# One attention layer over a graph: the mask merge moved to later steps, edge values on GpSimd, q2/k2 evictions at the end of a step

## The chip, the cores and the metric

The kernel runs on one core of a Trainium2 chip. The metric is the device time of one execution in microseconds (us), median of several runs. A profiled execution of the same program gives the trace that this text reads; its engines are PE (TensorE matmuls; PEld are its weight loads), ACT (ScalarE), DVE (VectorE), POOL (GpSimd) and SP, whose queue issues most transfers.

## The reference

384 nodes with 1024 features; 6528 edges, each with a type. The layer normalises, projects twice (q, k, v, then q2, k2, v2), adds an edge-type mask to the scores of 16 heads and adds its output to the input:

```python
h = jnp.maximum(_layernorm(x, axis=-1), 0.0)
q = h @ wq.T + bq                    # k and v likewise
q2 = (q @ wiq.T + biq).reshape(N, H, D).transpose(1, 0, 2)   # k2, v2 likewise
mask = jnp.full((N, N), -jnp.inf).at[src, dst].set(w[edge_type - 1])
mask = mask.at[idx, idx].set(jnp.where(jnp.isneginf(diag), w[3], diag))
scores = jnp.einsum('hnd,hmd->hnm', q2, k2) * scale + mask[None]
attn = jax.nn.softmax(scores, axis=-1)
out = jnp.einsum('hnm,hmd->hnd', attn, v2).transpose(1, 0, 2).reshape(N, OUT_F)
return x + out @ wo.T + bo
```

Here `w` is the softplus of four edge-type weights. Several edges may fall on one cell of the mask; the last one counts.

## The kernel before, in words

**Precision.** Every float32 operand is kept as a high part and a low part (`hi`, `lo`), and a product is made of three matmuls: hi·hi, hi·lo, lo·hi (`mm3`). So each weight chunk of 128x1024 that is loaded (`load`) is split: ACT copies the high part (`split_hi`, L77) and DVE or POOL subtracts it from the raw chunk for the low part (`split_lo`, L82).

**Weight steps.** There are 56 chunks; a step `w` works on chunk `w`. Steps 0 to 7 make v, 8 to 15 q, 16 to 23 v2, 24 to 31 k (the "k steps", `m` = 0 to 7), 32 to 47 alternate q2 and k2 for the eight pairs of heads, and the last eight chunks belong to the output projection `wo`. At the head of steps 0 to 31 `slot_head(w)` issues, in this order: the high split of chunk w+2, the evictions of the step before (`flush`, which runs what stands in `pend`), the low split of chunk w+2, the low parts that go with the evictions (`post`), the load of chunk w+4. An eviction of v, q or k is `evac_row`: DVE L381 scales the PSUM bank into `f`, ACT L382 writes the high part, DVE L383 the low part. In the k steps `v2_evac` is put into `pend` too: DVE L523, ACT L525, POOL L526. One of the three PSUM banks of tag `g` holds a v2 sum until its `v2_evac`, so that the k steps turn over the other two: step w writes the bank that step w-2 filled, and waits for that step's L381.

**The mask.** The edges are 51 columns of 128. Each edge's cell number is src·384+dst (`key`). So that the last edge of a cell wins, `mask_detect` (DVE L217) compares a column with its own row form and counts later edges on the same cell; `mask_index` (DVE L223, L224) turns cells that are overwritten later into a dump address, for a group of columns at once. `mask_values` makes each edge's value from its type, by nine small operations. `mask_scatter` (POOL L228) writes 128 values into one of three tables in DRAM by an indirect transfer; a table's next scatter waits for the landing of the one before. The detects and three scatters per step are spread over steps 0 to 19. In step 20 POOL reads the tables back (`mask_load`, L238), fills the mask tile `ma` (L140, L142) and writes its diagonal (`mask_base`, L210, L212). `mask_select` (DVE L242) lays one table over `ma`, by a predicated copy of 128x1152.

**Attention.** Steps of attention, `i` = 0 to 47, one for each third of a head, run as a pipeline over the engines. In step i PE makes the scores of i (`do_S`, L679), DVE adds the mask for i-1 (`do_ttr`, L685), ACT takes the exponential of i-2 (`do_exp`, L689), POOL normalises i-3 (`do_norm`, L694), PE transposes i-5 (`do_T`, L699), ACT and DVE evict the transpose of i-6 (`do_pt`, L708, L709), and every third step PE multiplies by v2 (`do_A`, L716), with `do_ao` and `do_aos` behind it (L726, L727, L731, L732). Between these PE is filled with the matmuls of q2 and k2, later with those of wo (`fill`). The work beside those matmuls, split and load of coming chunks and the eviction of a finished one (`qk_head`, `qk_done`: ACT L376, DVE L377, then transfers on SP), is put into a list `tasks`, which `run_tasks` empties once in each attention step. The splits of wo chunks 2 to 7 are issued by `wo_prep` at the ends of the attention steps in `WSTEPS`.

**What sets the order.** The schedule is manual: each engine runs its instructions in the order in which the program issues them, and waits at the first one that isn't ready. An instruction that stands early in the program therefore holds up all that its engine has behind it.

Of the kernel before, what the change touches and what calls it, by code (L numbers as in the profile page):

```python
# [12 lines left out]
OP = mybir.AluOpType  # L13
# [3 lines left out]
EC = E // 128  # L17
# [5 lines left out]
def gnn_kernel(ctx: ExitStack, tc: tile.TileContext, x, edges, erows, etw, wq, wk, wv, wiq, wik, wiv, wo,  # L23
# [6 lines left out]
    nc = tc.nc  # L30
# [6 lines left out]
    ctx.enter_context(tc.manual_schedule())  # L37

    EB = 8
    GI = 3  # L40
    NTAB, RNG = 3, EC // 3
    WARM = 20

    def bank(tag):
# [15 lines left out]
    def load(w):  # L60
        if w >= NCH:
            return
        n, m = chunks[w]
        raw[w] = wpool.tile([128, D], F32, tag="raw", name="raw", bufs=3)
        nc.sync.dma_start(raw[w], W[n][m])

    def split_hi(w, dst=None, dve=False):
        if w >= NCH:
            return
        if dst is None:  # L70
            t = wpool.tile([128, 2, D], F32R, tag="whl", name="whl", bufs=4)
            dst = (t[:, 0, :], t[:, 1, :])
        whl[w] = dst
        if dve:
            nc.vector.tensor_copy(dst[0], raw[w])
        else:
            nc.scalar.activation(dst[0], raw[w], AF.Copy)  # L77

    def split_lo(w, eng=None):
        if w < NCH:  # L80
            hi, lo = whl[w]
            (eng or nc.vector).tensor_tensor(lo, raw[w], hi.bitcast(F32), OP.subtract)  # L82

    def split(w, lo_eng=None, dst=None, hi_dve=False):
        split_hi(w, dst, hi_dve)
        split_lo(w, lo_eng)
# [32 lines left out]
    val = const.tile([128, EC], F32, name="val")  # L119
    idx = const.tile([128, EC], I32, name="idx")  # L120
    w8 = const.tile([128, 12], F32, name="w8")
# [8 lines left out]
    def mask_consts():  # L130
        nc.gpsimd.memset(upper, 1.0)
        nc.gpsimd.affine_select(upper, upper, pattern=[[1, 128]], compare_op=OP.is_gt, fill=0.0, base=0,
                                channel_multiplier=-1)
        nc.gpsimd.iota(dump.bitcast(I32), pattern=[[0, 1]], base=CELLS, channel_multiplier=1)
        nc.gpsimd.tensor_copy(w8[:, 8:9], dump.bitcast(I32))
        nc.gpsimd.memset(zero, 0.0)
# [7 lines left out]
    def table_clear(g):  # L144

        nc.sync.dma_start(tabs[g][:CELLS, :].rearrange("(j p m) o -> p j (m o)", p=128, m=N),
                          zero[:, None, :].to_broadcast([128, NT, N]))

    def mask_floats():
        nc.gpsimd.tensor_copy(ed.bitcast(F32), ed)  # L150

    def mask_keys():
        nc.gpsimd.tensor_scalar(tmpe[:, 0, :], tmpe[:, 0, :], float(N), None, op0=OP.mult)
        nc.gpsimd.tensor_tensor(key, tmpe[:, 0, :], tmpe[:, 1, :], OP.add)
# [5 lines left out]
    def softplus_b():  # L160
        nc.scalar.activation(w8[:, 4:8], w8[:, 4:8], AF.Exp)
        nc.scalar.activation(w8[:, 4:8], w8[:, 4:8], AF.Ln, bias=1.0)

        nc.scalar.activation(sq, epsc, AF.Exp)

    def softplus_c():
        nc.vector.tensor_tensor(w8[:, 4:8], w8[:, 4:8], w8[:, 0:4], OP.add)
        nc.vector.tensor_scalar(w8[:, 4:8], w8[:, 4:8], 8.0, 1.0e-37, op0=OP.mult, op1=OP.max)

    def mask_values():  # L170
        t, ty = tmpe[:, 0, :], tmpe[:, 2, :]
        nc.vector.tensor_scalar(val, ty, 0.0, w8[:, 7:8], op0=OP.is_equal, op1=OP.mult)
        for i in range(4):
            nc.vector.tensor_scalar(t, ty, float(i + 1), w8[:, 4 + i:5 + i], op0=OP.is_equal, op1=OP.mult)
            nc.vector.tensor_tensor(val, val, t, OP.add)

    krt = work.tile([128, N], F32, tag="e", name="kr", bufs=EB)
    kf = ert[:, :2 * EC]
# [1 line left out]
    def key_rows():  # L180

        nc.gpsimd.tensor_copy(kf, er)
        nc.gpsimd.tensor_scalar(kf[:, :EC], kf[:, :EC], float(N), None, op0=OP.mult)
        nc.gpsimd.tensor_tensor(krt[:, :EC], kf[:, :EC], kf[:, EC:], OP.add)
        nc.sync.dma_start(krow.rearrange("c j -> (c j)").rearrange("(p e) -> p e", p=128), krt[:, :EC])
# [10 lines left out]
    def key_load(g, s):  # L196

        if s == 0:
            t = work.tile([128, 2, NT, N], F32R, tag="pt", name="rows")
            krv[g] = t.bitcast(F32).rearrange("p a k n -> p (a k n)")  # L200
        c0, c1 = parts(g)[s]
        dst = krv[g][:, s * PA * 128:(s * PA + c1 - c0) * 128]
        for c in range(c0, c1):
            rows[c] = krv[g][:, (s * PA + c - c0) * 128:(s * PA + c - c0 + 1) * 128]
        nc.sync.dma_start(dst, krow[c0:c1, :].rearrange("c j -> (c j)").partition_broadcast(128))
# [14 lines left out]
    def mask_index(j0, j1):  # L220

        k, n, i, t0 = (a.rearrange("p (r j) -> p r j", r=NTAB)[:, :, j0:j1] for a in (key, cnt, idx, tmpe[:, 0, :]))
        nc.vector.scalar_tensor_tensor(t0, n, 2.0 * CELLS, k, op0=OP.mult, op1=OP.add)  # L223
        nc.vector.tensor_scalar(i, t0, w8[:, 8:9], None, op0=OP.min)  # L224
# [15 lines left out]
    def mask_select(g):  # L240

        nc.vector.copy_predicated(ma, mbt[g].bitcast(I32), mbt[g])  # L242
# [64 lines left out]
    def warm(n):  # L307
        for i in range(n):
            ps = bank("g")
            nc.tensor.transpose(ps[:, :128], ident, ident)  # L310

    mask_consts()
    warm(WARM)
    key_rows()
# [42 lines left out]
    ln_rstd()  # L357
    mask_floats()
    split(1, nc.gpsimd)
    softplus_b()  # L360
    softplus_c()
    mask_keys()


# [20 lines left out]
    w = 0  # L385
    pend, post = [], []

    def flush(last=False):
        while pend:
            pend.pop(0)()  # L390
        while last and post:
            post.pop(0)()

    def slot_head(w):
        split_hi(w + 2)
        if w != 1:
            flush()
        split_lo(w + 2, nc.gpsimd if w in (1, 2) else None)
        while post:
            post.pop(0)()  # L400
        load(w + 4)
# [26 lines left out]

    def detect(s):

        if s == 1:
            mask_values()
        if s < NTAB:
            table_clear(s)
        if 3 <= s < 6:
            key_load(1, s - 3)
        if 7 <= s < 10:
            key_load(2, s - 7)
        detects((0, 3, 6)[s] if s < 3 else 4)
        if s >= 3:  # L440
            scatters(3)
        if s == 14:
            biv_load()
# [3 lines left out]
    def detects(n):  # L447
        for i in range(nde[0], min(EC, nde[0] + n)):
            mask_detect(sc_order[i])
            if i % (NTAB * GI) == NTAB * GI - 1 or i == EC - 1:  # L450
                mask_index(i // (NTAB * GI) * GI, i // NTAB + 1)
            nde[0] = i + 1

    def extra_q(m):
# [4 lines left out]
    def scatters(n):  # L459
        for _ in range(n):  # L460
            if nsc[0] < EC:
                mask_scatter(nsc[0])
                nsc[0] += 1
# [64 lines left out]
    def extra_k(m):  # L528
        if 0 < m <= 6:
            pend.append(lambda: v2_evac(m - 1))  # L530
        for g in {0: (0, 1), 1: (2,)}.get(m, ()):
            mask_select(g)
        if m < 2:
            residual(m + 6)
    kT = gtile("g2")
# [31 lines left out]
    def run_tasks():  # L567
        while tasks:
            tasks.pop(0)()
# [27 lines left out]

    LT, LA = 5, 7
    PRE, RATE, RATE_O, RATE_E = 84, 7.9, 8, 8
    WSTEPS = (37, 38, 41, 44, 47, 51)  # L600
    PAR, OPOOL, ODVE = 1, (2, 3, 6), (2,)

    otile = {}
# [83 lines left out]
    def do_exp(i):  # L687
        s = sts[i]
        nc.scalar.activation(es[i], es[i], AF.Exp, bias=s[:, 0:1], scale=-1.0, accum_out=s[:, 1:2])  # L689
# [39 lines left out]
    def do_aos(h):  # L729
        p = h // 2  # L730
        nc.scalar.activation(ao[:, 0, p, :], aof[p], AF.Copy)  # L731
        nc.gpsimd.tensor_tensor(ao[:, 1, p, :], aof[p], ao[:, 0, p, :].bitcast(F32), OP.subtract)  # L732
# [19 lines left out]
    for i in range(S + LA + 4):  # L752
        now[0] = i
        r = RATE if len(gens) == 2 else RATE_O if i < S else RATE_E
        fill(r / 2)
        if i < S:
            do_S(i)
        fill(r / 2)
        if 0 <= i - 1 < S:
            do_ttr(i - 1)  # L760
        if 0 <= i - 2 < S:
            do_exp(i - 2)
        if 0 <= i - 3 < S:
            do_norm(i - 3)
        run_tasks()
        if 0 <= i - LT < S:
            do_T(i - LT)
        j = i - LA
        if j >= 2 and (j - 2) % 3 == 0 and (j - 2) // 3 < 16:
            do_A((j - 2) // 3)  # L770
        if 0 <= i - LT - 1 < S:
            do_pt(i - LT - 1)
        if j >= 3 and (j - 3) % 3 == 0 and (j - 3) // 3 < 16:
            do_ao((j - 3) // 3)
        if j >= 4 and (j - 4) % 6 == 3:
            do_aos((j - 4) // 3)
        if i == XSTEP:
            assert len(gens) < 2
            xb_load()
        if i in WSTEPS:  # L780
            wo_prep(wp)
            wready[wp] = i + 2
            wp += 1
# [57 lines left out]
```

## Time and profile before

| | us |
|---|---|
| median of 3 runs | 320.03 (319.42 to 320.71) |
| the profiled execution | 318.8 |
| span of its trace | 317.1 |
| PE busy in it | 297.0 (94%) |
| DVE busy | 204.3 (64%) |
| POOL busy | 166.5 (53%) |
| ACT busy | 154.8 (49%) |

The span runs from the first to the last instruction of the program; 1.7 us of the execution's time lie around it. A busy share is an average over stages of different kinds, so that PE's idle 20 us have to be looked for by place. The trace also tells the clock that was granted to PE, as a share of full speed.

### The profile page before, as it was taken

The numbers are of one execution on the slowest core, as the hardware profiler recorded it, in microseconds if no ns is written. First come the engines' busy times: TensorE is split into PE (matmuls) and PEld (weight loads), VectorE is DVE, ScalarE is ACT, GpSimd is POOL, SyncE is SP. The second block draws the span as 40 slices with busy tenths as digits, with TensorE's granted clock in tenths as the row PEclk, the third lists the DMA queues.
The fourth block names the chain that finished last, engine by engine and source line by source line (L and its number), as shares of the span: only waits on it lengthen the run. The fifth ranks groups of instructions, "written<-read, shape, count | busy, mean of one in ns | idle before, by whom it ended". The sixth has DMA issues, their size and how long they took to land.

```text
span 317.1 us, 4954 instructions
## 1 busy us (share of the span) xinstructions
PE 297.0 (94%) x1643; PEld 279.4 (88%) x1643; DVE 204.3 (64%) x494; ACT 154.8 (49%) x286; POOL 166.5 (53%) x163
## 2 busy tenths in 40 slices
PE   6699999999999995499999999999999999699995
PEld 5699999999888894499999999999999898588884
DVE  2979999986534320999933666666565657796413
ACT  3693434533422220255453567686776758676200
POOL 4654567775767666033333347282837365857010
PEclk9599999999999998599999999999999999999999
DMA  7899567545495559233348975647474626900005
GB/s 226 267 271 360 171 208 246 183 136 199 146 291 196 159 177 353 93 137 131 102 144 205 272 199 143 180 113 196 120 193 115 192 64 166 366 34 0 2 0 198
DMA packets 22377, 55.12 MB, mean 174 GB/s; under 512 B 4816, under 2 KB 8400, under 8 KB 22352
## 3 DMA queue, kind: packets, MB, share of 16 engines
q1 hardware_dynamic: 20288, 53.01, 54.6%
q0 software_dynamic: 2064, 1.80, 1.9%
q8 instruction: 13, 0.21, 0.3%
q14 instruction: 12, 0.10, 0.1%
HBM read 40.39 MB, written 4.97 MB: 143 GB/s over the span
## 4 chain that ended last, share of the span: by engine, by line
PE 69%; DMA 12%; issue 6%; POOL 6%; DVE 3%; ACT 3%; SPq 0%; DVEq 0%; POOLq 0%
PE g L366 17%; PE g L368 17%; PE g L367 17%; DMA tab<-val,idx 10%; PE a L716 5%; PE s L679 4%; PE t L699 4%; POOL tab L228 3%; DMA g<-in_x_dram 2%; PE g L412 2%; POOL e L694 1%; ACT nat L376 1%; DVE whl L82 1%; DVE pt L709 1%; ACT e L689 1%
## 5 line engine op out<-in xcount | busy, mean ns | idle before, releaser
L366 PE MATMUL g<-g,whl 128*128 128x384 f32 x312 | 107.3, 344 | 8.2 <-DVE f L381 8.2
L368 PE MATMUL g<-g,whl 128*128 128x384 f32 x312 | 105.3, 337 | 0.0
L367 PE MATMUL g<-g,whl 128*128 128x384 f32 x312 | 105.0, 336 | 0.0
L228 POOL DMA_INDIRECT tab<-val,idx x51 | 58.2, 1141 | 31.5 <-DMA tab<-val,idx 12.1
L366 PEld LDWEIGHTS g<-g,whl 128*128 128x128 f32 x312 | 59.3, 190 | 8.5 <-issue 8.5
L694 POOL TENSOR_TENSOR e<-e,s 128x384 f32<-128x384 f32 x48 | 40.2, 846 | 49.0 <-DVE s L693 43.1
L77 ACT ACTIVATE whl<-raw 128x1024 fp32r<-128x1024 f32 x51 | 53.3, 1049 | 23.3 <-PE g L368 21.1
L367 PEld LDWEIGHTS g<-g,whl 128*128 128x128 f32 x312 | 59.3, 190 | 0.0
L368 PEld LDWEIGHTS g<-g,whl 128*128 128x128 f32 x312 | 59.1, 189 | 0.0
L82 DVE TENSOR_TENSOR whl<-raw,whl 128x1024 fp32r<-128x1024 f32 x39 | 47.6, 1221 | 13.5 <-ACT whl L77 13.5
L382 ACT ACTIVATE g<-f,bc 128x384 fp32r<-128x384 f32 x24 | 14.8, 617 | 65.6 <-DVE f L381 65.6
L82 POOL TENSOR_TENSOR whl<-raw,whl 128x1024 fp32r<-128x1024 f32 x13 | 32.0, 2460 | 17.5 <-ACT whl L77 13.0
L377 DVE SCALAR_TENSOR_TENSOR nat<-g,bc,nat 128x384 fp32r<-128x384 f32 x16 | 9.9, 618 | 36.3 <-ACT nat L376 36.3
L689 ACT ACTIVATE e<-e,s 128x384 f32<-128x384 f32 x48 | 29.4, 613 | 7.8 <-DVE s L685 7.0
L709 DVE TENSOR_TENSOR pt<-t,pt 128x384 fp32r<-128x384 f32 x48 | 26.4, 549 | 4.7 <-ACT pt L708 4.2
L685 DVE CUSTOM_DVE_ANT_0 e<-s,ma 128x384 f32<-128x384 f32 x48 | 26.3, 549 | 4.0 <-PE s L679 3.8
L699 PE MATMUL t<-ident,e 128*128 128x128 f32 x144 | 23.7, 273 | 3.4 <-POOL e L694 2.6
L708 ACT ACTIVATE pt<-t 128x384 fp32r<-128x384 f32 x48 | 23.1, 482 | 6.4 <-PE t L699 5.4
L679 PE MATMUL s<-ks,qs 128*128 128x384 f32 x96 | 25.2, 343 | 0.2
L699 PEld LDWEIGHTS t<-ident,e 128*128 128x128 f32 x144 | 18.2, 140 | 7.7 <-POOL e L694 3.2
L376 ACT ACTIVATE nat<-g,bc 128x384 fp32r<-128x384 f32 x16 | 9.3, 582 | 26.2 <-PE g L368 20.2
L383 DVE SCALAR_TENSOR_TENSOR g<-f,bc,g 128x384 fp32r<-128x384 f32 x24 | 20.9, 872 | 0.8 <-ACT g L382 0.8
(147 smaller groups left out, 431.7 us busy)
## 6 DMA issues: line engine op xcount, KB each, us to landing
ks<-nat SPq DMA_DIRECT2D x32, 192.0 KB, 3.5
raw<-in_wv_dram SPq DMA_DIRECT2D x8, 512.0 KB, 5.6
raw<-in_wq_dram SPq DMA_DIRECT2D x8, 512.0 KB, 3.7
raw<-in_wiv_dram SPq DMA_DIRECT2D x8, 512.0 KB, 3.4
raw<-in_wk_dram SPq DMA_DIRECT2D x8, 512.0 KB, 4.6
raw<-in_wiq_dram SPq DMA_DIRECT2D x8, 512.0 KB, 3.4
raw<-in_wik_dram SPq DMA_DIRECT2D x8, 512.0 KB, 4.7
raw<-in_wo_dram SPq DMA_DIRECT2D x8, 512.0 KB, 4.9
```

The costliest lines, as they stand in the source:

```text
L77: nc.scalar.activation(dst[0], raw[w], AF.Copy)
L82: (eng or nc.vector).tensor_tensor(lo, raw[w], hi.bitcast(F32), OP.subtract)
L228: nc.gpsimd.indirect_dma_start(out=tabs[c // RNG], out_offset=bass.IndirectOffsetOnAxis(ap=idx[:, c:c + 1], axis=0), in_=val[:, c:c + 1], ...
L366: nc.tensor.matmul(ps, lhi, rhi, start=first, stop=False)
L367: nc.tensor.matmul(ps, lhi, rlo, start=False, stop=False)
L368: nc.tensor.matmul(ps, llo, rhi, start=False, stop=last)
L679: nc.tensor.matmul(ps[:, :N], qs[:, o, t * 128:(t + 1) * 128], ks[:, o, s, :], start=(s == 0), stop=(s == 1))
L685: nc.vector.tensor_tensor_reduce(e, st_ps.pop(i)[:, :N], ma[:, t, :], -0.125, 3.0e38, OP.add, OP.min, s[:, 0:1])
L689: nc.scalar.activation(es[i], es[i], AF.Exp, bias=s[:, 0:1], scale=-1.0, accum_out=s[:, 1:2])
L694: nc.gpsimd.tensor_tensor(es[i], es[i], s[:, 2:3].to_broadcast([128, N]), OP.mult)
L699: nc.tensor.transpose(ps[:, k * 128:(k + 1) * 128], es[i][:, k * 128:(k + 1) * 128], ident)
L709: nc.vector.tensor_tensor(lo, pv, hi.bitcast(F32), OP.subtract)
```

## The change

Five edits, in the order of the program:

- The high split of chunk 2 is issued before the operations of the softplus (`softplus_b`), no more at the head of step 0; the two DVE operations of `softplus_c` move into step 0, behind the low split of chunk 2.
- `mask_values` runs on POOL in step 0 (it ran on DVE in step 1), and the low splits of chunks 3 and 4 run on DVE (they ran on POOL).
- The groups of `mask_index` end at columns 1, 3, 5, 8, 11, 14, 17 of each table (they ended at 3, 6, 9, 12, 15, 17), and five detects instead of six belong to step 2.
- `mask_select` for the three tables is issued in k steps 4, 5 and 6 (two were issued in k step 0, one in k step 1).
- `run_tasks` stands behind `do_aos` at the end of an attention step (it stood between `do_norm` and `do_T`). In `WSTEPS` the second and third wo split move from steps 38 and 41 to 40 and 42.

PE's instructions stand in the same order in both kernels.

```diff
-    GI = 3
+    JI = [0, 1, 3, 5, 8, 11, 14, RNG]
...
     def mask_values():
-        nc.vector.tensor_scalar(val, ty, 0.0, w8[:, 7:8], op0=OP.is_equal, op1=OP.mult)
+        nc.gpsimd.tensor_scalar(val, ty, 0.0, w8[:, 7:8], op0=OP.is_equal, op1=OP.mult)
         for i in range(4):
-            nc.vector.tensor_scalar(t, ty, float(i + 1), w8[:, 4 + i:5 + i], op0=OP.is_equal, op1=OP.mult)
-            nc.vector.tensor_tensor(val, val, t, OP.add)
+            nc.gpsimd.tensor_scalar(t, ty, float(i + 1), w8[:, 4 + i:5 + i], op0=OP.is_equal, op1=OP.mult)
+            nc.gpsimd.tensor_tensor(val, val, t, OP.add)
...
     split(1, nc.gpsimd)
+    split_hi(2)
     softplus_b()
-    softplus_c()
...
     def slot_head(w):
-        split_hi(w + 2)
+        if w > 0:
+            split_hi(w + 2)
         if w != 1:
             flush()
-        split_lo(w + 2, nc.gpsimd if w in (1, 2) else None)
+        split_lo(w + 2)
...
     def detect(s):
-        if s == 1:
+        if s == 0:
+            softplus_c()
             mask_values()
...
-        detects((0, 3, 6)[s] if s < 3 else 4)
+        detects((0, 3, 5)[s] if s < 3 else 4)
...
             mask_detect(sc_order[i])
-            if i % (NTAB * GI) == NTAB * GI - 1 or i == EC - 1:
-                mask_index(i // (NTAB * GI) * GI, i // NTAB + 1)
+            if i + 1 == NTAB * JI[1]:
+                mask_index(JI.pop(0), JI[0])
...
-        for g in {0: (0, 1), 1: (2,)}.get(m, ()):
-            mask_select(g)
+        if 4 <= m < 7:
+            mask_select(m - 4)
...
-    WSTEPS = (37, 38, 41, 44, 47, 51)
+    WSTEPS = (37, 40, 42, 44, 47, 51)
...
             do_norm(i - 3)
-        run_tasks()
         if 0 <= i - LT < S:
             do_T(i - LT)
...
             do_aos((j - 4) // 3)
+        run_tasks()
         if i == XSTEP:
```

## The prediction

> **What bounds the kernel now.** I read the page's busy times and slices first, then PE's waits, then the time lines of the engines named there. PE is busy 94% of the span, and its order doesn't change, so only its idle time and its slow clock can be won.
>
> ```profile
> PE   6699999999999995499999999999999999699995
> ...
> PEclk9599999999999998599999999999999999999999
> ```
>
> Each digit is 7.9 us. Beside the first two slices there is one hole, in slices 15 and 16 (119 to 135 us), and the clock falls to half in the same place. Near slice 34 lies a smaller hole. PE's waits name them:
>
> ```profile
> PE g L366 <- DVE f L381: 8.2, 1, 8.2
> ...
> PE t L699 <- POOL e L694: 2.6, 2, 1.7
> ...
> PE t L699 <- DVE pt L709: 0.8, 1, 0.8
> ```
>
> (Columns: us in total, times, longest.) The 8.2 us are one wait of k step 2 for an eviction on DVE. DVE's time line says what DVE did then:
>
> ```profile
> 112.47 1.22 DVE L82 TENSOR_TENSOR whl<-raw,whl 128x1024 fp32r<-128x1024 f32 x1
> 127.14 2.90 DVE L242 COPY_PREDICATED ma<-mbs 128x1152 f32<-128x1152 int32 x2 [13.45 <-POOL ma L212]
> 129.94 0.68 DVE L495 TENSOR_TENSOR xh<-xh,bot 128x512 f32<-128x512 f32 x1
> 130.53 0.55 DVE L381 TENSOR_TENSOR f<-g,rrow 128x384 f32<-128x384 f32 x1
> ```
>
> DVE stood 13.45 us in front of the first mask copy, which waited for POOL's L212; the eviction L381 of k step 0 was ready at 118.7 but queued behind it. POOL in turn came late through its 51 scatters (34.1 to 117.4) and the read-back:
>
> ```profile
> 116.41 0.96 POOL L228 DMA_INDIRECT tab<-val,idx  x1 [0.30 <-issue]
> ...
> 121.71 0.75 POOL L238 DMA_DIRECT2D mbs<-tab  x1 [2.54 <-DMA tab<-val,idx]
> ...
> 126.66 0.45 POOL L212 TENSOR_TENSOR ma<-ma,d 128x128 f32<-128x128 f32 x1
> ```
>
> **The mask copies in k steps 4 to 6.** *Removed:* PE's last matmul before the hole starts at 122.72; at its pace of 0.173 us the next would start at 122.89, and starts at 131.23: 8.34 us. *The clock:* from 131.23 to 135.46 PE starts 13 matmuls at half clock in 4.23 us; at full clock 13 x 0.173 = 2.25, so 1.98 us more. The Trainium skill ("TensorE: Matmul & The Clock Gate", the HAM clock gate) states that an idle window of about 3.4 us halves the clock and a busy one of as much restores it; 3.4 us at half speed would cost 1.7. I take the row, 1.98. Both go only if no new hole of that length comes. Sum 10.3.
>
> *Is the mask ready?* A step is 24 x 0.173 = 4.16 us. Without the hole steps 26, 27, 28 end at 127.05, 131.2, 135.4. The first copy stands on DVE behind the head of k step 4 (step 28), so it is reached at about 135.3, while POOL's L212 was done at 127.1 even at its old pace. An earlier test: the third v2 eviction (L523, head of step 28, reached at 132.0) reuses a buffer that POOL's first L526 must have read, and that stands behind L212: 127.1 + 1.53 = 128.6. So POOL may be 3.4 us later than before without harm.
>
> *Does DVE bear the copies there?* Its work in such a step of before goes from one L381 to the next, 134.08 to 137.84:
>
> ```profile
> 134.08 0.54 DVE L381 TENSOR_TENSOR f<-g,rrow 128x384 f32<-128x384 f32 x1
> ...
> 135.13 1.21 DVE L82 TENSOR_TENSOR whl<-raw,whl 128x1024 fp32r<-128x1024 f32 x1
> 136.27 1.65 DVE L383 SCALAR_TENSOR_TENSOR g<-f,bc,g 128x384 fp32r<-128x384 f32 x1
> 137.84 0.55 DVE L381 TENSOR_TENSOR f<-g,rrow 128x384 f32<-128x384 f32 x1
> ```
>
> L383 takes 1.65 here, but 0.61 at 132.13 where POOL is idle; POOL's L526 runs from 135.96 to 137.50. "GPSIMD Engine Reference" (key points) says that POOL contends with DVE instructions that have two SBUF inputs: a rule against this change, since L383 and the copies are such. With 0.61 a step would need 3.76 - 1.04 + 1.43 = 4.15 us with a copy, just one step of PE, and no lag. With the row, 3.76 + 1.43 = 5.19: DVE falls back 1.03 in each of three steps, 3.1 in all. I take the row. The copies themselves follow L383, when POOL is through, so they keep their 1.43 (two of before; 1.52 the third). What is late next: L381 of step 30 starts 0.3 + 3.1 after that step's end and takes 0.55, done at +3.95; step 32 needs its bank at +4.16. Stall 0, with 0.2 in hand; each 0.1 us on the copies adds 0.3. With copies of 1.52 it is 0.1, with copies stretched by as much as L383 (+1.0 each) 2.8. I take 0, range 0 to 2.8. In step 31 a v2 eviction frees the third bank, and DVE has time again.
>
> **The early steps** lie beside PE, whose matmuls run without a gap from 21.4 to 122.7 while DVE lags it by up to 6 us. DVE loses nine operations that held it from 23.17 to 29.04 (two of them took 1.73 and 2.39 beside POOL's L82) and gains two low splits, 2 x 1.22. On POOL, rows of 128x51 take 0.35 to 0.38 (tensor with scalar) and 0.29 to 0.30 (two tensors): 5 x 0.38 + 4 x 0.30 = 3.1, about 4 with gaps; in exchange two splits of 2.4 leave. New waits: the values wait for DVE's softplus operations, which now stand behind the low split of chunk 2 and ACT's logarithm, ending about 20.5, so POOL has the values at 24.5; behind them wait only scatters. The first L223 on DVE waits for those values (shared scratch), with L381 of step 1 and the low split of chunk 4 behind it; DVE reaches it at about 25, and chunk 4 is needed at 31.6. Even values twice as slow would fit. On SP the loads and table clears of steps 0 and 1 wait for low splits that end 1 to 2 us earlier. The first scatter moves from 34.1 to about 26 and the fourth, which needs the second group, from 38.3 to about 32; POOL's chain ends some 6 us earlier. That adds to the margin above and buys no time: 0. Bounds -0.3 to +0.5, as PE has steps of slack.
>
> **`run_tasks` at the end of the step.** The chain of waits shows what it costs now:
>
> ```profile
> 246.46 0.59 ACT nat L376
> ...
> 247.61 0.39 DVE whl L82
> ...
> 248.74 0.56 DVE pt L709
> ...
> 249.44 0.52 PE t L699 x3
> ```
>
> ACT waited for the last matmul of a chunk (to 246.44), with `do_pt` queued behind on ACT and DVE, whose bank PE's transposes needed: PE's start-to-start 248.35 to 249.44 is 1.09, so 0.9 lost. The same chain through L685 costs about 0.3 (0.39 and 0.28 between starts instead of 0.17) at 204.9, 219.9 and 234.8. With the tasks last, `do_pt` and `do_ao` fill the wait: 0.5 to 1.0 us earlier for DVE, which is what these holes need. Gain 1.8, bounds 0 to 1.8. What gets later by some 1.5 us is the tasks' own work: POOL's low split (2.4) in front of a normalisation that PE needs two steps (5 us) on, the loads on SP (needed two chunks on), and the stack transfers, whose pair is four steps ahead (84 matmuls before the first step, then 7.9 a step against 8 needed). These cost 0 so long as that lead stands; a lead of nothing would cost about 1 us for each of 13 tasks.
>
> **The wo splits.** POOL, from its time line:
>
> ```profile
> 265.14 2.41 POOL L82 TENSOR_TENSOR whl<-raw,whl 128x1024 fp32r<-128x1024 f32 x1 [4.57 <-PE t L699]
> 267.51 0.83 POOL L694 TENSOR_TENSOR e<-e,s 128x384 f32<-128x384 f32 x1
> ...
> 269.27 2.39 POOL L82 TENSOR_TENSOR whl<-raw,whl 128x1024 fp32r<-128x1024 f32 x1
> 271.62 4.94 POOL L694 TENSOR_TENSOR e<-e,s 128x384 f32<-128x384 f32 x5
> ```
>
> PE lost 2.06 and 1.21 at 270.4 and 273.1, waiting for these L694, 2.9 beyond its pace. With the second split two steps later the L694 of steps 39 and 40 run at 269.3 and 270.1, the split from about 270.9 to 273.3, and the next L694 ends at 274.1 instead of 275.0; PE's third transpose then starts at 274.2 instead of 276.05. So 1.8 at best; the third split's DVE part may meet that L694, which before stretched one to 1.8. I take 1.5, bounds 0 to 2. The matmuls with these chunks are held to step 44 anyway, and SP's loads wait for the same low splits.
>
> **Sum.** 8.34 + 1.98 + 1.8 + 1.5 = 13.6. Against the profiled execution: 318.8 - 13.6 = 305.2. The median shown is 1.2 above that execution, so 306.4.
>
> **Rivals.** *A, the attention edits give nothing (15%):* the delays they take away were other engines' load and come back a step later. Only 10.3: 309.7. Against it: ACT's wait is for PE, not load. *B, DVE's lag makes a new hole (8%):* copies contended by 1 us stall 2.8, with part of the half clock coming back and a share of the attention gain lost: 310 to 313. For it: L383's 1.65; against: POOL has no work during the copies. *C, slower (4%):* with the tasks last, the stacks come too late for the scores and PE waits at each of the 13 heads between 186 and 260. It decides above 13.6/13 = 1.05 us a head; at 1.5 us, 320 + 5.9 = 326. Against: the lead of four steps. *D, no change (2%):* the hole moves whole to step 28, because POOL finishes 11 us later than before: 319 to 321. Against: its first scatter can only be earlier. The forecast keeps 71%, own range 305 to 308.5.
>
> A measurement here can tell about 0.5% (1.6 us) from no change. Range for 8 in 10: 304.6 to 310.5, with A and the near end of B in it. Faster 0.94, within 0.5% 0.02, slower 0.04.
>
> **What would show it.** PE's wait for L381 gone, clock full after the first slices; copies of 1.4 to 1.5 at about 135, 140 and 145 with no wait on POOL; first scatter near 26; no start-to-start of PE over 0.5 us between 186 and 260 of before's time. Wrong if step 32 waits for L381, if L685 or the scores wait for stacks, or if POOL's L694 still holds PE for 3 us near the wo splits.

## The result, and the profile after

The changed kernel takes 305.76 us (median of six runs, 305.07 to 307.93); the kernel before, run on the same chip, takes 320.82. The ratio is 0.954 [0.950, 0.958]. The profiled execution took 305.34 us with a span of 303.6, so 13.5 us less span than before. The forecast was 306.4 (304.6 to 310.5): time and sign are right. The sum is right too (13.6 forecast, 13.5 found), but some of its terms are not, and they happen to cancel. In the runs below a few single executions lie over 1.5% above the fastest of their kernel; medians and ranges count them, ratios leave them out.

Busy share of PE and its clock in 40 slices of 7.6 us, from the page of the kernel after:

```profile
PE   7699999999999999999997999999999999999995
...
PEclk9799999999999999999999999999999999999999
```

The hole of slices 15 and 16 is gone, and so is the half clock in it. A small dent is new, in slice 21 (about 163 us). PE's waits in the kernel after name it (columns: us in total, times, longest; from the k steps on, lines stand two further down than before, so the scores are L681, the transposes L701, the normalisation L696, and the addition to a block of x L497):

```profile
PE s L293 <- ACT g L281: 3.0, 2, 2.2
PE s L681 <- DMA ks<-nat: 1.7, 1, 1.7
PE g L310 <- POOL ident masks.py:199: 1.4, 1, 1.4
PE t L701 <- DVE pt L711: 0.3, 1, 0.3
```

The 8.2 us for L381 and the 2.6 us for POOL's normalisation have left the list. The second line is new: the first scores wait for the first k2 stack. The first and third belong to the start of the kernel and stood there before.

PE runs the same 1643 matmuls in the same order in both kernels, so the traces can be laid over one another matmul by matmul. Wherever the distance of the two start times changes, something was won or lost:

| where | forecast | measured (us) |
|---|---|---|
| k step 2, hole | -8.34 | -8.33 |
| half clock behind it | -1.98 | -1.99 |
| DVE's lag, first scores of attention | 0 | +1.93 |
| heads of attention (`run_tasks`) | -1.8 | -1.8 |
| wo splits | -1.5 | -2.1 |
| prologue, first 50 matmuls | 0 | -1.2 |
| sum | -13.6 | -13.5 |

The measured column is one pair of executions. Of the 1.93 at the first scores 1.85 is the wait itself and 0.08 a longer start of the matmul behind it. The prologue's 1.2 is not the change's: 0.3 is an earlier arrival of x, and 0.85 is a half clock that lasted 6.83 us in the profiled execution of before and 3.41 in this one. In the executions of the other kernels this half clock lasted 0, 3.41 or 6.83 us, with no relation to their edits.

### The profile page after: what moved, and what is told of

It is laid out like the page before. It is cut to its first block, busy times and chain, and to the rows that moved or that the text cites. A ratio compares the mean times of both kernels' runs of the same rounds, so it can differ in the third digit from the quotient of the medians.

```text
span 303.6 us, 4945 instructions
## 1 busy us (share of the span) xinstructions
PE 293.4 (97%) x1643; PEld 276.8 (91%) x1643; DVE 201.6 (66%) x489; ACT 154.5 (51%) x286; POOL 163.4 (54%) x170
## 4 chain that ended last, share of the span: by engine, by line
PE 90%; DMA 4%; SPq 2%; ACT 2%; DVE 1%; issue 0%; ACTq 0%
PE g L368 20%; PE g L366 20%; PE g L367 20%; PE s L681 6%; PE a L718 6%; PE t L701 5%; DMA g<-in_x_dram 2%; DMA ks<-nat 2%; PE s L366 2%; PE s L367 2%; PE s L368 2%; PE t L368 2%; PE t L367 2%; PE t L366 2%; PE g L413 1%; PE a L366 1%
## 5 line engine op out<-in xcount | busy, mean ns | idle before, releaser
L228 POOL DMA_INDIRECT tab<-val,idx x51 | 55.6, 1091 | 28.9 <-DMA tab<-val,idx 13.3
L696 POOL TENSOR_TENSOR e<-e,s 128x384 f32<-128x384 f32 x48 | 40.2, 849 | 42.2 <-DVE s L695 32.3
L82 DVE TENSOR_TENSOR whl<-raw,whl 128x1024 fp32r<-128x1024 f32 x41 | 50.4, 1230 | 12.6 <-ACT whl L77 12.6
L367 PEld LDWEIGHTS g<-g,whl 128*128 128x128 f32 x312 | 58.7, 188 | 0.0
L366 PEld LDWEIGHTS g<-g,whl 128*128 128x128 f32 x312 | 58.6, 188 | 0.0
L368 PEld LDWEIGHTS g<-g,whl 128*128 128x128 f32 x312 | 58.5, 188 | 0.0
L382 ACT ACTIVATE g<-f,bc 128x384 fp32r<-128x384 f32 x24 | 14.9, 620 | 57.7 <-DVE f L381 57.7
L82 POOL TENSOR_TENSOR whl<-raw,whl 128x1024 fp32r<-128x1024 f32 x11 | 26.5, 2408 | 15.8 <-ACT whl L77 12.1
L687 DVE CUSTOM_DVE_ANT_0 e<-s,ma 128x384 f32<-128x384 f32 x48 | 26.3, 550 | 6.1 <-PE s L681 6.0
L681 PE MATMUL s<-ks,qs 128*128 128x384 f32 x96 | 25.4, 345 | 1.7 <-DMA ks<-nat 1.7
L701 PE MATMUL t<-ident,e 128*128 128x128 f32 x144 | 23.5, 272 | 0.3 <-DVE pt L711 0.3
L701 PEld LDWEIGHTS t<-ident,e 128*128 128x128 f32 x144 | 18.7, 140 | 3.4 <-issue 0.6
L377 DVE SCALAR_TENSOR_TENSOR nat<-g,bc,nat 128x384 fp32r<-128x384 f32 x16 | 9.9, 618 | 17.5 <-ACT nat L376 13.5
L383 DVE SCALAR_TENSOR_TENSOR g<-f,bc,g 128x384 fp32r<-128x384 f32 x24 | 20.9, 876 | 0.7 <-ACT g L382 0.7
L718 PE MATMUL a<-pt,vhl 128*128 128x384 f32 x96 | 20.8, 351 | 0.0
```

The costliest lines, as they stand in the source:

```text
L228: nc.gpsimd.indirect_dma_start(out=tabs[c // RNG], out_offset=bass.IndirectOffsetOnAxis(ap=idx[:, c:c + 1], axis=0), in_=val[:, c:c + 1], ...
L366: nc.tensor.matmul(ps, lhi, rhi, start=first, stop=False)
L367: nc.tensor.matmul(ps, lhi, rlo, start=False, stop=False)
L368: nc.tensor.matmul(ps, llo, rhi, start=False, stop=last)
L681: nc.tensor.matmul(ps[:, :N], qs[:, o, t * 128:(t + 1) * 128], ks[:, o, s, :], start=(s == 0), stop=(s == 1))
L696: nc.gpsimd.tensor_tensor(es[i], es[i], s[:, 2:3].to_broadcast([128, N]), OP.mult)
```

## The experiments

**One part alone.** Four kernels put one part of the change into the kernel before. They ran with before on one chip (321.06 us there).

*The mask copies alone:*

```
-        for g in {0: (0, 1), 1: (2,)}.get(m, ()):
-            mask_select(g)
+        if 4 <= m < 7:
+            mask_select(m - 4)
```

> The kernel before with one edit: the mask copies in k steps 4 to 6. Theory (the hole before k step 2 is DVE's queue behind the copies, and the copies now make DVE late, which makes the stacks of the first scores late): hole of 8.3 us and half clock of 2.0 gone, 1.8 given back at the first scores, so 8.5 us faster, about 312. Rival (the new wait at the first scores comes from another edit): the full 10.3, about 310.5. Second rival (POOL's old late chain still holds the copies): a new hole at k steps 4 to 6, 316 or more.

310.43 us (308.96 to 320.97), ratio 0.967 [0.961, 0.973]. In its trace PE wins 8.33 and 1.99 at the same two places. PE's waits, mask copies alone:

```profile
PE t L699 <- POOL e L694: 2.6, 2, 1.7
...
PE s L679 <- DMA ks<-nat: 1.3, 1, 1.3
PE t L699 <- DVE pt L709: 0.8, 1, 0.8
PE g L366 <- DVE f L381: 0.7, 1, 0.7
```

The attention's waits stay as they were, and two new ones come with the copies: one for L381 (PE's loss at step 32 is 0.92) and the one at the first scores (1.57). So the moved copies bring the new wait; the edits in attention don't. The median lies where the rival had it (310.5), but the trace decides for the theory: 10.3 won, 2.5 given back. It also gives 1.1 in the prologue and takes 1.55 by a half clock late in attention (at 265.7 us), neither of which comes from the edit.

*The tasks alone*, in the loop over the attention steps:

```
-        run_tasks()
...
+        run_tasks()
```

> The kernel before with run_tasks at the end of the step alone. Theory: four small holes of PE between 200 and 250 go, 1.8 us faster, about 319. Rival (the lateness of the tasks' own work is paid elsewhere): 0, or slower by up to 1 us, with waits for stacks or for normalised scores in their place.

315.42 us (313.91 to 317.92), ratio 0.985 [0.979, 0.991], more than the forecast 1.8. PE's waits, tasks alone:

```profile
PE g L366 <- DVE f L381: 8.5, 1, 8.5
...
PE t L699 <- POOL e L694: 0.7, 1, 0.7
```

The hole stays. The trace shows the forecast 1.8 (0.19, 0.18, 0.37 and 0.93 at the four heads, 0.1 at one before them), and as much again (1.7) in the region of the wo splits: the wait for POOL's L694 falls from 2.6 to 0.7, although the splits are where they were. POOL starts the first wo split at 262.18 instead of 265.14, 3.0 us earlier, while PE itself runs only 1.8 earlier there: with the tasks last the split gains 1.2 us on PE.

*The wo splits alone:*

```
-    WSTEPS = (37, 38, 41, 44, 47, 51)
+    WSTEPS = (37, 40, 42, 44, 47, 51)
```

> The kernel before with the wo splits at steps 40 and 42 alone. Theory: PE's two holes at 270 to 274 shrink by 1.5 to 2.0 us, about 319. Rival (the holes are ACT's or DVE's load in steps without filling matmuls, and POOL's split only happens to stand there): 0 to 0.5 us.

318.77 us, ratio 0.996 [0.990, 1.002]: no difference that can be measured. The trace wins 1.89 and 0.59 at the two old holes and loses 1.59 at a new one. Chain of waits, wo splits alone:

```profile
271.94 1.34 POOL whl L82
...
274.31 1.81 POOL e L694
...
276.17 0.55 PE t L699 x3
```

The second split still stands in front of a normalisation that PE needs, only later. Alone the edit is worth about 0.9, not the 1.5 of the forecast. The medians can't show it: in this execution the hole of k step 2, where nothing was edited, was 1.8 us longer than in the trace of before.

*The early edits alone:* the high split of chunk 2, the softplus, the values, the low splits, the groups and the detects as in the change, of which these are the lines that matter here:

```
-            nc.vector.tensor_tensor(val, val, t, OP.add)
+            nc.gpsimd.tensor_tensor(val, val, t, OP.add)
...
-        split_lo(w + 2, nc.gpsimd if w in (1, 2) else None)
+        split_lo(w + 2)
...
-            if i % (NTAB * GI) == NTAB * GI - 1 or i == EC - 1:
-                mask_index(i // (NTAB * GI) * GI, i // NTAB + 1)
+            if i + 1 == NTAB * JI[1]:
+                mask_index(JI.pop(0), JI[0])
```

> The kernel before with the early edits alone (edge values on POOL, low splits of chunks 3 and 4 on DVE, softplus moved, smaller first groups of cell numbers); mask copies in k steps 0 and 1. The changed kernel's POOL had the mask base ready at 120.6 instead of 127.1. Theory: the copies then end near 123.5, L381 of k step 0 near 124.8 instead of 131.1, so the hole shrinks from 8.3 to about 3 us and may stay under the length that halves the clock: 5 to 7 us faster, 313 to 316. Rival, as the prediction had it (these edits buy no time by themselves): within 1 us of before.

Inconclusive: 313.49 to 331.64 us. In the profiled execution PE ran for 20 us at half clock around 88 to 108 us, with pauses that no wait of an engine explains. The kernel was run again later.

**What the early edits are worth.** The same kernel as in the last experiment, once more:

> The kernel before with the early edits alone, a second time, since the first time's executions lay too far apart. Theory: POOL's mask base ends near 120.6, the copies near 123.5 and L381 of k step 0 near 124.8, so the hole shrinks from 8.3 to about 3 us and the half clock may go: 5 to 7 us faster than before. Rival, as the prediction had it: within 1 us of before.

309.73 us (308.43 to 314.66) against 319.12 for before on that chip, ratio 0.972 [0.964, 0.979]. So the early edits alone, for which the forecast has nothing, also take most of the hole away. POOL's time line and then DVE's, early edits alone:

```profile
116.39 0.46 POOL L212 TENSOR_TENSOR ma<-ma,d 128x128 f32<-128x128 f32 x1
```

```profile
116.88 3.15 DVE L242 COPY_PREDICATED ma<-mbs 128x1152 f32<-128x1152 int32 x2 [0.83 <-POOL ma L212]
122.26 0.69 DVE L497 TENSOR_TENSOR xh<-xh,bot 128x512 f32<-128x512 f32 x1 [2.22 <-DMA xh<-in_x_dram]
122.86 0.55 DVE L381 TENSOR_TENSOR f<-g,rrow 128x384 f32<-128x384 f32 x1
```

POOL's last L212 ends at 116.85, 10.3 us earlier than before (the last scatter starts at 105.06 instead of 116.41). The copies, still at their old place, wait 0.83 instead of 13.45. What is left of the hole, 1.5 us for L381, has another cause: L381 stands behind an addition for which a block of x arrives at 122.2. PE wins 6.7 at the hole and 1.9 of half clock.

*The change without its early edits* (the lines above taken back, in the kernel after):

> The changed kernel without the early edits (edge values on DVE in step 1, groups of three, splits and softplus as before); mask copies, run_tasks and wo splits as changed. Theory, as the prediction had it (the early edits only add margin): within 0.5 us of the changed kernel, POOL's mask base at 127 and the copies at 134 without a wait. Rival (without the earlier scatters POOL's chain holds the v2 evictions or the copies): a hole in the k steps, 1 to 4 us slower than the changed kernel.

305.70 us (305.26 to 308.33), ratio 0.962 [0.955, 0.968]; the whole change on the same chip took 305.49 (ratio 0.961 [0.952, 0.970], the run below). The hole and its half clock are gone (8.33 and 1.99). POOL has the mask's base ready at 127.7, and the first copy starts at 135.3 without a wait, as the theory had it. So in the medians the early edits buy nothing beside the moved copies, and beside the early edits the moved copies buy only the rest of the hole: each of the two takes the same wait away. The profiled execution loses 2.0 more than the change behind k step 2: 0.2 at step 32, 0.2 in the wait at the first scores and 1.6 in a half clock behind that wait. Whether the early edits spare this is open, with one trace.

**Where the 1.9 us at the first scores come from.** The theory: DVE leaves the k steps late by its three copies, this delays the eviction of the last k step and the high splits behind it on ACT, these the low split and the load of chunk 37 on SP, and that load, the first q2 stack behind it and the next load share the DMA engines with the first k2 stack. The chain of waits of the kernel after, from the end of step 32 to the first scores:

```profile
151.04 0.72 ACT whl L77
...
151.79 1.24 DVE whl L82
...
153.04 0.33 SPq L65
...
155.98 0.53 SPq L65
...
156.55 0.47 SPq L564
...
158.35 5.66 DMA ks<-nat
...
164.14 0.58 PE s L681 x2
```

L65 is the load of a weight chunk, L554 the first of the four transfers of the q2 stack, L564 a transfer of the k2 stack. SP's time line before:

```profile
161.83 0.33 SPq L65 DMA_DIRECT2D raw<-in_wik_dram  x1
163.20 0.54 SPq L552 DMA_DIRECT2D qs<-nat  x1
...
165.76 0.54 SPq L65 DMA_DIRECT2D raw<-in_wiq_dram  x1
168.01 3.66 SPq L562 DMA_DIRECT2D ks<-nat  x4
```

The two loads are issued at 153.04 and 155.98, around PE's end of step 33 (155.2). Before, step 33 ended at 166.7: the first load was 4.9 us ahead of that end and is now 2.2. The q2 stack started 4.8 us ahead of the k2 stack and now 3.1. The first two stack transfers were issued at 168.01 and 168.52 and landed 4.0 us later, at 172.0 and 172.5, before PE came to the scores at 173.8. Now they take 6.6 and 6.9 us and land at 163.1 and 164.0, and PE, which could start at 162.3, waits. The second load is stretched too, from 3.6 us to 6.2.

*The rivals* were that the tasks' new place makes the stack late, which the mask copies alone refute (the tasks stand at their old place there, and the wait is there), and that PE now comes earlier than the DMA queue can serve, whatever DVE does. First the whole change once more, as the base for this chip:

> The changed kernel once more, to stand beside the next three on one chip: about 306, ratio 0.954 to before, with PE waiting 1.5 to 2 us at the first scores if that wait is no accident of one execution.

305.49 us (303.7 to 307.39), with the same wait (1.93 lost at the first scores).

*The copies moved out of the k steps*, into the heads of chunks 33 to 35, behind the low split:

```
-        if 4 <= m < 7:
-            mask_select(m - 4)
...
         split_lo(w + 2, nc.gpsimd if (w + 2) % 2 == PAR else None)
+        if W0 < w < W0 + 4:
+            mask_select(w - W0 - 1)
```

> The changed kernel with the three mask copies issued behind the heads of chunks 33, 34 and 35 (the first q2 and k2 chunks), where DVE has gaps of 1.5 us or more, no more in k steps 4 to 6. Theory (DVE's lag of 3.1 us delays the low split of chunk 34, so the load of chunk 37 starts late and competes with the transfers of the first k2 stack): DVE doesn't lag, the first k2 stack lands 4 us after its issue instead of 6.6 to 7.4, the first scores don't wait, 1.8 us faster than the changed kernel. Rival (the stacks are late because PE now reaches them earlier than the DMA queue can serve, whatever DVE does): the wait at the first scores stays, 0.

304.12 us (303.43 to 306.22), ratio to before 0.959 [0.951, 0.967]. ACT's time line in the change, and then with the copies moved on:

```profile
150.18 0.62 ACT L382 ACTIVATE g<-f,bc 128x384 fp32r<-128x384 f32 x1 [2.52 <-DVE f L381]
150.71 1.99 ACT L77 ACTIVATE whl<-raw 128x1024 fp32r<-128x1024 f32 x2
...
155.25 0.58 ACT L376 ACTIVATE nat<-g,bc 128x384 fp32r<-128x384 f32 x1 [1.13 <-issue]
```

```profile
147.90 0.62 ACT L382 ACTIVATE g<-f,bc 128x384 fp32r<-128x384 f32 x1 [2.93 <-DVE f L381]
148.42 1.99 ACT L77 ACTIVATE whl<-raw 128x1024 fp32r<-128x1024 f32 x2
...
155.68 0.58 ACT L376 ACTIVATE nat<-g,bc 128x384 fp32r<-128x384 f32 x1 [2.63 <-issue]
```

The last L376 follows the end of step 33 in both. Ahead of it the last k step's L382 stood 5.07 us in the change and stands 7.78 here, as it did before (158.97 to 166.75). PE's waits, copies moved on, from the second line to the end of the list:

```profile
PE g L310 <- POOL ident masks.py:199: 1.4, 1, 1.4
PE t L701 <- DVE pt L711: 0.3, 1, 0.3
```

The wait for the stack is gone and, behind the prologue, the rest of PE's start times is as in the change. That shows the first link of the theory, the copies on DVE, and refutes the second rival: PE comes to the scores as early as in the change. The same kernel on another chip:

> The changed kernel with the mask copies behind the heads of chunks 33 to 35, timed in more rounds. Theory: as before its trace has no wait at the first scores; 1.5 to 2 us below the changed kernel, 0.949 to 0.955 of the kernel before.

304.17 us (302.26 to 304.7, seven runs; before 319.12), ratio 0.955 [0.951, 0.959]. So this kernel beats the one before. Against the change its traces show the 1.93 gone; the medians on the chip where both ran (304.12 and 305.49) point the same way by 1.4, but their ranges overlap, so that the times alone don't show it.

*The load of chunk w+4 behind the stack's transfers on SP* tests the last link, the sharing:

```
     def qk_head(w):
-        load(w + 4)
         split_hi(w + 2)
         if pendq:
             pendq.pop(0)()
+        load(w + 4)
```

> The changed kernel with the load of chunk w+4 issued behind the stack transfers in the head of a q2 or k2 chunk, not ahead of them; DVE's lag stays. Theory (two weight loads of 512 KB compete with the first k2 stack): one of the two now follows the stack, which lands 1 to 2 us earlier: 1.0 to 1.8 us faster than the changed kernel. Rival (the DVE lag alone delays the stack): 0. If a load comes too late for its split: slower by up to 1 us, with PE or ACT waiting for raw chunks.

307.76 us (307.2 to 310.01), ratio to before 0.968 [0.962, 0.975]: 2.3 us above the change in the medians, with ranges that just overlap. PE's waits, load last:

```profile
PE s L681 <- DVE s L687: 1.9, 1, 1.9
...
PE s L681 <- DMA ks<-nat: 0.8, 1, 0.8
```

PE's loss in the wait for the stack falls by 0.85, from 1.93 to 1.08, as less stands in its way; but now a raw chunk comes late (its load takes 7.44 us, to 168.52), its high split, the eviction behind it on ACT and the mask addition L687 follow, PE loses 2.1 at a later score, and 1.5 more at half clock. In one order the stack is late, in the other a raw chunk. So the last link is shown only in part. In the traces that tell the landing, the first transfer of the k2 stack took 6.0 to 6.7 us where it was issued 3.5 us behind the load of chunk 37 (four traces) and 2.6 to 4.6 us where it was issued 5.0 to 6.2 us behind it (five traces). That the transfers stretch one another is read from this; no run took the loads away.

**The margin of DVE.** Each copy issued twice in the change:

```
         if 4 <= m < 7:
             mask_select(m - 4)
+            mask_select(m - 4)
```

> The changed kernel with each mask copy made twice in its k step (the second changes nothing). It sizes DVE's margin in the k steps. Theory (5.2 us a step with one copy, 0.2 us in hand at step 32): 3 x 1.43 more, so PE waits 4.1 us for L381 in steps 31 and 32 together, and the wait of 1.8 at the first scores stays: 4 us slower, about 310; with part of the half clock 311 to 312. Rival (DVE has slack that its lag doesn't show): under 2 us slower.

310.80 us (309.74 to 311.54), ratio to before 0.977 [0.971, 0.983]. DVE's time line in a k step, and PE's wait, copies twice:

```profile
141.06 3.02 DVE L242 COPY_PREDICATED ma<-mbs 128x1152 f32<-128x1152 int32 x2
143.97 0.55 DVE L381 TENSOR_TENSOR f<-g,rrow 128x384 f32<-128x384 f32 x1
```

```profile
PE g L366 <- DVE f L381: 4.0, 2, 2.2
```

The change itself did not run on this chip. The lag of steps 29 and 30 now reaches PE two steps later, in steps 31 and 32: 4.0 us of waits where the model of the forecast gives 4.1. The wait for the stack, which the expectation kept, has vanished, since PE comes to the scores later; it does not add to the other. A half clock of 3.4 us follows the second wait.

**The wo splits taken back out of the change** (the old `WSTEPS`):

```
-    WSTEPS = (37, 40, 42, 44, 47, 51)
+    WSTEPS = (37, 38, 41, 44, 47, 51)
```

> The changed kernel with the wo splits back at steps 38 and 41. The prediction gave this edit 1.5 us, bounds 0 to 2: slower than the changed kernel by that, about 307. Theory after the single edits (run_tasks at the end of the step alone already shortened the holes near the wo splits by 1.6 us): slower by 0 to 0.5 us, about 306.

307.81 us (305.63 to 308.87), ratio 0.964 [0.958, 0.971]. The change itself did not run on this chip, and its ratios elsewhere (0.954 and 0.961) have intervals that reach this one's or nearly so. Little of the difference lies in the wo region. Laid over the change's trace, this execution is 3.5 us longer: 1.1 in the prologue, 0.2 at step 32, 0.3 in the wait for the stack and 1.6 in a half clock behind it. In the wo region it loses 0.9 at one start and gets half of it back: 0.4 net, which is what the edit is worth beside the tasks' move, by this one trace.

## Why the prediction was right, step by step

- **The hole and the clock (10.3): right,** 8.33 and 1.99. The copies ran at 134.0, 139.2 and 144.4 (forecast 135, 140, 145) and waited for nothing. The condition "only if no new hole of that length comes" was put at a length that is too long: pauses of PE of 2.23 us brought the half clock back in other kernels (the last section). The change's new pause, 2.03 us, didn't, and part of that is luck. DVE's time line in the kernel after:

```profile
134.01 1.55 DVE L242 COPY_PREDICATED ma<-mbs 128x1152 f32<-128x1152 int32 x1
135.44 0.55 DVE L381 TENSOR_TENSOR f<-g,rrow 128x384 f32<-128x384 f32 x1
...
139.21 1.55 DVE L242 COPY_PREDICATED ma<-mbs 128x1152 f32<-128x1152 int32 x1
140.63 0.56 DVE L381 TENSOR_TENSOR f<-g,rrow 128x384 f32<-128x384 f32 x1
...
144.41 1.55 DVE L242 COPY_PREDICATED ma<-mbs 128x1152 f32<-128x1152 int32 x1
145.83 0.56 DVE L381 TENSOR_TENSOR f<-g,rrow 128x384 f32<-128x384 f32 x1
```

- **"DVE falls back 1.03 in each of three steps": right.** From one L381 to the next are 5.19 and 5.20 us. The choice of the row with POOL beside it (L383 at 1.65) over the free 0.61 was the right one: L383 took 1.64 to 1.67 in all these steps. "Stall 0, with 0.2 in hand" held in the change: the last L381 above ends at 146.39, and step 32 starts at 146.68. With the mask copies alone it cost 0.9, because there the first v2 eviction had waited 1.63 us for a store of x and DVE came to the copies already late. The margin was as thin as the forecast said.
- **"What is late next": this is the step that failed.** The forecast followed the lag to the bank of step 32 and stopped there ("in step 31 ... DVE has time again"). DVE does catch up, but the weight loads behind it are issued 2.7 us nearer to the first stack, and this costs 1.93. The sentence on the stacks, "these cost 0 so long as that lead stands", asked only whether the tasks' move would eat the lead; the mask copies ate it. "The scores wait for stacks" stood among the forecast's own signs of being wrong, and that sign came, at the first head.
- **`run_tasks` (1.8): right,** 1.67 at its four places and 0.1 at a head before them. Its effect on the wo region, another 1.7 when it stands alone, was missed.
- **The wo splits (1.5): the region's gain is 2.1, but the edit's own share is 0.4.** Alone it gives 0.9, and beside the tasks' move 0.4; the tasks' move alone relieves the same waits. The mechanism was the forecast one. POOL's time line in the kernel after:

```profile
254.94 0.83 POOL L696 TENSOR_TENSOR e<-e,s 128x384 f32<-128x384 f32 x1
...
256.69 1.62 POOL L696 TENSOR_TENSOR e<-e,s 128x384 f32<-128x384 f32 x2
258.43 2.38 POOL L82 TENSOR_TENSOR whl<-raw,whl 128x1024 fp32r<-128x1024 f32 x1
260.76 3.46 POOL L696 TENSOR_TENSOR e<-e,s 128x384 f32<-128x384 f32 x3
```

  Three normalisations now run between the first split (252.58) and the second; before, one did.
- **The early edits (0): right for the change, for a reason that holds only in it.** Values took 5.1 us on POOL (19.9 to 25.0; forecast about 4, and twice that allowed for; five operations took 0.47 to 0.50 where the forecast put 0.38, and one of the others 1.16); the first scatter starts at 26.34 (forecast 26), the fourth at 33.44 (32), and the mask's base is ready at 120.6, 6.5 us earlier (6). That end differs by several us from execution to execution, however: 116.0 to 124.2 us in eight traces of kernels with the early edits (111.8 in the one with 20 us of half clock ahead of it), 123.5 to 128.0 in five without. "That adds to the margin above and buys no time" is true beside the moved copies. Alone the same 6 to 10 us shorten the hole itself, and about 9 us of time go.
- **The rivals.** B had the right suspect, DVE's lag, at the wrong place. C had the right victim, the stacks, but through the tasks and at every head; there is one wait, at the first head, and it costs 1.9 us. A is refuted by the 3.9 us that the attention region gives, D by the hole's being gone.

So that the sum came out to 0.1 us is luck: the unforecast wait (+1.9) met a shorter prologue (-1.2), which is no effect of the change, and a wo region that gave 0.6 more.

## What to carry to other kernels

When an engine is allowed to fall back because its results are not needed yet, follow the lag past the next consumer to everything that the same engine's work releases, loads and their place among other transfers too, until it has caught up. Test parts of a change both alone and left out: two edits that each remove the same wait look worth the whole gain alone and nothing beside one another. And put bulk work where the engine stands idle for longer than the work lasts: the same three copies cost 1.9 us in the k steps and nothing five steps later.

## What the runs showed of the hardware

- **In these traces the clock halves by PE's idle time within a fixed stretch of 3.41 us, and that can be well under the whole stretch.** The forecast weighed the Trainium skill's "TensorE: Matmul & The Clock Gate" (the HAM clock gate), with its idle window of about 3.4 us. Here a half clock of 3.41 us followed single pauses of 2.23 (the change without early edits), 2.28 (load last), 2.28 (old wo splits) and 2.59 us (copies twice), measured from start to start. In attention and the k steps none followed pauses of 1.67 to 2.07 us, except once (mask copies alone), behind two pauses of 2.05 and 1.21 close together. Before, and in both executions of the early edits alone, such a pair (2.03 to 2.07 and 1.21) did nothing.

  The place of the pauses explains this. Within one execution the changes of the clock lie whole multiples of 3.413 us apart (before: at 9.06, 15.88, 125.11 and 135.35 us, that is 2, 32 and 3 of them). Cut each trace into these stretches and add up what PE's pauses take of each (distances of starts over 0.3 us, less the 0.17 of a matmul). In the 14 traces a half clock followed all 20 full-clock stretches with 2.04 us or more of pauses, and none of the others, some 1,180, which have 1.94 or less. The two pauses fall into one stretch with the mask copies alone (2.24 us), and into two before (1.27 and 1.65). PE's stretches, mask copies alone and then before (columns: stretch; length; busy time of PE, PEld, DVE, ACT and POOL with their instructions; clock granted; busy share of DMA, GB/s; the ends of PE's matmuls are modelled):

```profile
262.33:265.74 3.41, 1.33 (x9) 1.02 (x10) 3.02 (x7) 2.36 (x6) 3.41 (x4) 1.00 1.01 393
265.74:269.16 3.42, 3.42 (x14) 3.33 (x13) 1.50 (x5) 1.80 (x6) 1.87 (x3) 0.50 1.00 405
```

```profile
268.47:271.88 3.41, 2.30 (x13) 1.70 (x11) 1.78 (x6) 2.48 (x6) 3.41 (x3) 1.00 0.86 291
271.88:275.29 3.41, 1.92 (x12) 1.61 (x13) 3.13 (x8) 2.27 (x7) 3.41 (x4) 1.00 1.02 400
```

  The change's own pause of 2.03 us at the first scores was cut by such a boundary in one execution (0.79 and 1.07) and fell into one stretch in the other (1.86), just short of enough. Each half clock in attention or the k steps cost 1.5 to 1.6 us (the forecast's estimate from the page's window was 1.7), so a wait that grows by 0.2 us can cost 1.8 more. No run varied the pause alone.
- **The start of the program differs between executions:** by 0.8 us in the two traces of the change, by 1.6 in the two with the copies moved on, and in all from 0.5 us later to 2.4 earlier than the profiled execution of before, with 0, 3.41 or 6.83 us at half clock in the first 17 us. A difference of that size in one pair of traces says nothing on an edit further down.
- **A predicated copy of 128x1152 took 1.55 us in the k steps of the change,** with 1.42 to 1.43 from its start to that of the next instruction; the three took 1.43, 1.43 and 1.52 before. Moved behind the heads of chunks 33 to 35, they took 1.72, 3.75 and 1.53. The 3.75, the same in both of these traces, stands beside a low split on POOL. Time lines of DVE and of POOL, copies moved on:

```profile
157.96 3.75 DVE L242 COPY_PREDICATED ma<-mbs 128x1152 f32<-128x1152 int32 x1
```

```profile
157.28 3.01 POOL L82 TENSOR_TENSOR whl<-raw,whl 128x1024 fp32r<-128x1024 f32 x1 [4.30 <-ACT whl L77]
```

  This fits the rule on POOL and DVE that the forecast weighed: the copies can be stretched, though in the k steps none was. PE lost nothing by it. No run took the split away.
